# Walking the adjacency matrix by 512-column chunks instead of by row strips in a four-layer graph network kernel

## The chip, the cores and the metric

The kernel runs on one core of one Trainium2 chip, in one launch. The metric is the device time of that launch in microseconds (us), as a median of several executions; 2% either way counts as a difference. Times inside a kernel come from one profiled execution each and count from the start of its span.

The engines go by their short names: PE makes the matrix products (PEld is its loading of weights) into the accumulator banks called PSUM, DVE and ACT work on vectors, POOL issues the gathers of rows here, and SP the other transfers.

## The reference

`x` has 2708 rows of 128 features, `adj` is 2708 x 2708, all float32. Cut to what matters:

```python
def layer0(x, A):                       # neighbours in feature space are added to A
    z = leaky_relu(lap_mul(A, x) @ W1 + b1)          # pass 1 over adj
    S = exp(-sqrt(dist2(z, z)) / 2); keep the 4 nearest of each row
    return lap_mul(S + A, x) @ W2 + b2               # pass 2 over adj
def layer1(X, A):                       # attention over the graph
    den = exp(leaky_relu(s_row[:, None] + s_col[None, :]))
    att = den / (A @ den)
    return A @ (att @ (X @ W))                       # a last pass over adj
layer2: normalised adj @ x, then W;  layer3: adj @ x, concat, W, relu
# each layer: x = layernorm(x + layer(x, adj))
```

The kernel computes `A @ den` cheaply: it ranks the nodes by `s_col`, and splits each row's sum by blocks of ranks into a product with block sums (the *carry* pass over adj) and a part from gathered rows of adj inside a block (the *own section*). The ranking is what end_layer0 and the rank stage below prepare.

## The kernel before: the parts concerned

The matrix is cut into 22 row tiles of 128 and 6 chunks of 512 columns (the last has 148). Six row tiles stay in the on-chip buffer (`res`), 16 are streamed again in every pass, through three buffers. Tile's scheduler decides at build time in which order each engine runs its instructions. The code is shortened, and partly put in words.

```python
def load_strip(rows):                      # 128 x 2708, 1354 KB, tag "strip", bufs=3
    s = stream.tile([P, N], F32, tag="strip", name="strip")
    nc.sync.dma_start(s[...], adjT[rows * P : ..., :])
    return s

def adj_times(y, done, extra=None, lead=()):
    accs = [acc_tile() for _ in range(C)]             # six PSUM accumulators at once
    for n, i in enumerate(streamed tiles):            # 16 strips, six products each
        src = load_strip(i)
        for c in range(C): add(c, i, src, n == 0, False)
    for c in range(C):                                # then chunk by chunk
        for i in range(S, T): add(c, i, res[:, i - S, :], ...)
        if extra is not None: extra(c, accs[c])
        nc.scalar.copy(hT[:, chunk c], accs[c])
        done(c, chunk_tiles[c])                       # work on the chunk's four node tiles

# pass 2: the 88 gathers of neighbour rows (four per node tile) and their weighted sums
for t in range(T):
    for k in range(TOPK):
        got = got_pool.tile([P, D], F32, tag="got")   # bufs=16
        nc.gpsimd.indirect_dma_start(out=got, in_=y2_rows, in_offset=where[:, t, k])
        near_sum[:, t, :] (+)= got * sim[:, t, k]     # DVE
def add_near(c, acc):  ...                            # near_sum of four tiles into acc, on PE
def end_layer0(c, ts): ...                            # linear, layernorm, scores, and the
    # masks: each tile's scores are compared with those of all earlier nodes (DVE),
    # and the masks are summed on PE into rk
adj_times(y2, end_layer0, extra=add_near)
# ... rank stage: positions, block sums lc, xws gathers, rows_from(csort), rows_from(rr) ...
# carry: six accumulators at once, evacuated at the end
# ... own section: 2 x 43 gathers of rows of adj into "strip" buffers ...
adj_times(mixed, end_layer1); adj_times(y3, end_layer2); adj_times(xs, end_layer3)
```

PSUM: 6 banks `acc` and 2 banks `mis`; `rk` takes an acc bank. Below, *end c* is end_layer0 of chunk c, timed by its first step on DVE; *rank* is the start of the rank stage; `csort` and `rr` are groups of small transposes on PE in that stage, and `xws` are rows gathered there, which ACT scales.

Of the kernel before, what the change touches and what calls it, by code (L numbers as in the profile page):

```python
# [8 lines left out]
F32 = mybir.dt.float32  # L9
# [7 lines left out]
P = 128  # L17
CW = 512
# [11 lines left out]
def kernel(  # L30
# [16 lines left out]
    nc = tc.nc  # L47
    N, D = x.shape
    assert D == P
    T = (N + P - 1) // P  # L50
    C = (N + CW - 1) // CW
    FULL = N // P
    LAST = N - FULL * P
    NQ = T
    S = T - RES
    NB = (N + BJ - 1) // BJ
    HALF = N // 2
    pw = [min(P, N - t * P) for t in range(T)]
    cw = [min(CW, N - c * CW) for c in range(C)]

    chunk_tiles = [range(c * 4, min(T, c * 4 + 4)) for c in range(C)]
# [3 lines left out]
    stream = ctx.enter_context(tc.tile_pool(name="stream", bufs=3))  # L65
    small = ctx.enter_context(tc.tile_pool(name="small", bufs=3))
    psum = ExitStack()
    acc_pool = psum.enter_context(tc.tile_pool(name="acc", bufs=6, space=bass.MemoryType.PSUM))
    mis_pool = psum.enter_context(tc.tile_pool(name="mis", bufs=2, space=bass.MemoryType.PSUM))
    dram = ctx.enter_context(tc.tile_pool(name="dram", bufs=1, space=bass.MemoryType.DRAM))  # L70

    def acc_tile():
        return acc_pool.tile([P, CW], F32, tag="acc", name="acc")
# [4 lines left out]
    def load_strip(rows):  # L78
        s = stream.tile([P, N], F32, tag="strip", name="strip")
        nc.sync.dma_start(s[: pw[rows], :], adjT[rows * P : rows * P + pw[rows], :])  # L80
        return s


    res = big.tile([P, RES, N], F32, tag="res", name="res")
# [40 lines left out]
    def evacuate(n, dst, src):  # L125
        if n % 2:
            nc.scalar.copy(dst, src)
        else:
            nc.vector.tensor_copy(dst, src)

    def adj_times(y, done, extra=None, lead=()):



        lead = dict(lead)
        accs = [acc_tile() for _ in range(C)]

        def add(c, i, src, first, last):
            nc.tensor.matmul(  # L139
                accs[c][:, : cw[c]], lhsT=y[: pw[i], i, :], rhs=src[: pw[i], c * CW : c * CW + cw[c]],  # L140
                start=first, stop=last,
            )

        for n, i in enumerate(list(lead) + [i for i in range(S) if i not in lead]):
            src = lead[i] if i in lead else load_strip(i)
            for c in range(C):
                add(c, i, src, n == 0, False)
        for c in range(C):
            for i in range(S, T):
                add(c, i, res[:, i - S, :], False, i == T - 1 and extra is None)  # L150
            if extra is not None:
                extra(c, accs[c])
            nc.scalar.copy(hT[:, c * CW : c * CW + cw[c]], accs[c][:, : cw[c]])  # L153
            done(c, chunk_tiles[c])

    def inv_sqrt(dst, src):
        nc.scalar.activation(dst, src, AF.Sqrt)
# [148 lines left out]
    with tc.tile_pool(name="knn", bufs=1) as knn:  # L306
# [46 lines left out]
        def weigh(ts):  # L353

            t0, t1 = ts[0], ts[-1] + 1
            nr, sm = near[:, t0:t1, :TOPK], sim[:, t0:t1, :]

            nc.vector.tensor_add(nr, nr, nsq[:, t0:t1, None].to_broadcast([P, t1 - t0, TOPK]))
            nc.vector.tensor_scalar(nr, nr, 0.0, DIST_EPS, op0=ALU.min, op1=ALU.subtract)
            nc.scalar.activation(sm, nr, AF.Sqrt, scale=-1.0)  # L360
            nc.scalar.activation(sm, sm, AF.Exp, scale=-0.5)
            dd = d2inv[:, t0:t1]
            nc.vector.tensor_reduce(dd, sm, AX.X, ALU.add)
            nc.vector.tensor_add(dd, dd, deg[:, t0:t1])
            inv_sqrt(dd, dd)
            scale_rows(y2, xs, d2inv, ts)
            full = min(t1, FULL)
            nc.sync.dma_start(
                y2_rows[t0 * P : full * P, :].rearrange("(t p) d -> p t d", p=P), y2[:, t0:full, :]
            )  # L370
            if full < t1:
                nc.sync.dma_start(y2_rows[FULL * P :, :], y2[:LAST, FULL, :])

        with tc.tile_pool(name="keys", bufs=3) as keys:
            for t in range(T):
                p = pw[t]
                z2 = small.tile([P, P], F32, tag="z", name="z2")
                nc.scalar.mul(z2[:, :p], zT[:, t * P : t * P + p], 2.0)

                key = keys.tile([P, N], F32, tag="key", name="key")  # L380
                pks = [acc_tile() for _ in range(C)]
                for c in range(C):
                    cs = slice(c * CW, c * CW + cw[c])
                    nc.tensor.matmul(pks[c][:p, : cw[c]], lhsT=ones3[:, :p], rhs=nsq3[:, cs], start=True, stop=False)  # L384
                for c in range(C):
                    cs = slice(c * CW, c * CW + cw[c])
                    nc.tensor.matmul(pks[c][:p, : cw[c]], lhsT=z2[:, :p], rhs=zT[:, cs], start=False, stop=True)  # L387
                    nc.scalar.copy(key[:p, cs], pks[c][:p, : cw[c]])  # L388
                nc.vector.max(near[:p, t, :], key[:p])  # L389
                nc.vector.max_index(where[:p, t, :], near[:p, t, :], key[:p])  # L390
                if t == T - 6:
                    weigh(range(0, T - 5))
            weigh(range(T - 5, T))


    wide = ctx.enter_context(tc.tile_pool(name="wide", bufs=1))
# [22 lines left out]
    def add_near(c, acc):  # L419
        ts = chunk_tiles[c]  # L420
        for t in ts:
            p = pw[t]
            o = t * P - c * CW
            nc.tensor.matmul(
                acc[:, o : o + p], lhsT=near_sum[:p, t, :], rhs=ident[:p, :p], start=False, stop=(t == ts[-1])
            )
# [14 lines left out]
    rows_d = atile([T], "rows_d")  # L441
    nc.vector.memset(rows_m, 0.0)
    add_bias(b2_sb)
    rk = None

    def end_layer0(c, ts):
        nonlocal rk
        for t in ts:
            p = pw[t]
            po = linear(t, w2_sb)  # L450
# [1 line left out]
                xs[:p, t, :], po[:p, :D], d2inv[:p, t : t + 1], xs[:p, t, :], op0=ALU.mult, op1=ALU.add  # L452
            )
        normalize(ts, xs)
        if rk is None:
            rk = acc_tile()
        for t in ts:
            p, o = pw[t], t * P
            pt = mis_tile()
# [29 lines left out]
                accum_out=rows_d[:p, t : t + 1],  # L489
            )  # L490

    adj_times(y2, end_layer0, extra=add_near)
    late.close()
    lwx = ctx.enter_context(tc.tile_pool(name="lwx", bufs=1))
    xws = lwx.tile([P, NQ, D], F32, tag="xws", name="xws")
# [164 lines left out]
                haccs[:, o:e], lhsT=xws[:p, q, :], rhs=err[:p, o:e], start=(q == 0), stop=(q == NQ - 1)  # L660
            )

    accs = [acc_tile() for _ in range(C)]
    for n, i in enumerate(range(T)):
        src = load_strip(i) if i < S else res[:, i - S, :]
        for c in range(C):
            nc.tensor.matmul(  # L667
                accs[c][: 2 * NB, : cw[c]],
                lhsT=lc[: pw[i], i, :, :].rearrange("p b s -> p (b s)"),
                rhs=src[: pw[i], c * CW : c * CW + cw[c]],  # L670
                start=(n == 0), stop=(n == T - 1),
            )
    for c in range(C):
        evacuate(c, carry[: 2 * NB, c * CW : c * CW + cw[c]], accs[c][: 2 * NB, : cw[c]])
    psum.close()
    adj_half = adjT.rearrange("n (h k) -> (n h) k", h=2)
    WIDE = 2 * CW
# [67 lines left out]
                        mix(w, q, num, h * HALF + c0, hacc[:, c0 : c0 + w], own)  # L745
                nc.scalar.copy(mT[:, h * HALF : (h + 1) * HALF], hacc[:, :HALF])

    acc_pool = ctx.enter_context(tc.tile_pool(name="acc2", bufs=6, space=bass.MemoryType.PSUM))
    mis_pool = ctx.enter_context(tc.tile_pool(name="mis2", bufs=2, space=bass.MemoryType.PSUM))

    mixed = big.tile([P, T, D], F32, tag="y", name="mixed")
    for t in range(T):
# [18 lines left out]
            nc.scalar.mul(y3[: pw[t], t, :], xs[: pw[t], t, :], dinv[: pw[t], t : t + 1])  # L771
            nc.gpsimd.tensor_add(xs[: pw[t], t, :], xs[: pw[t], t, :], bl_sb[: pw[t]])

    adj_times(mixed, end_layer1)


    own3 = big.tile([P, T, D], F32, tag="y", name="own3")
# [7 lines left out]
            )  # L785
        normalize(ts, xs)

    adj_times(y3, end_layer2)

    for t in range(T):  # L790
        p = pw[t]
# [21 lines left out]
        if t1 <= ts[-1]:  # L813
            nc.sync.dma_start(out[FULL * P :, :], last[:LAST, FULL, :])

    adj_times(xs, end_layer3)


# [32 lines left out]
```

## Time and profile before

The median was 1321.56 us (1320.59 to 1323.04). PE is busy for 83% of the profiled span, DVE for 51%, POOL for 18%. By stages (from the profiled execution of 1338.7 us):

| stage | from, us | length, us | what ends last there |
|---|---|---|---|
| degrees, pass 1, neighbour search | 0 | 365 | not changed |
| pass 2 while neighbours are gathered | 365 | 146 | the 88 gathers on POOL |
| end_layer0, six chunks | 511 | 96 | DVE and PE in turn |
| rank and carry | 607 | 156 | DVE, then PE |
| own section | 763 | 227 | PE |
| layers 1 to 3 | 990 | 347 | PE, 93 to 100% busy |

Such a table is made by looking for the first or last instruction that writes a named tile, and asking for the busy time of every engine in the stretch between. The prediction shows the lines.

### The profile page before, as it was taken

How to read it: one execution, taken by the hardware profiler on the slowest of the kernel's cores; microseconds unless marked ns; L12 is line 12 of the kernel's file. 1: busy time of each engine (PE TensorE's matmuls, PEld its weight loads, DVE VectorE, ACT ScalarE, POOL GpSimd, SP SyncE). 2: the span in 40 equal slices, each digit the busy share in tenths (PEclk: the TensorE clock that was granted, in tenths of full speed). 3: DMA queues.
4: the chain of work that ended last, by engine and by line, in shares of the span. 5: the costliest groups of instructions: out<-in, count | busy, mean ns of one | idle time of the engine just before them, and what ended most of it. 6: DMA issues, size and time to landing. Idle time of an engine off the chain costs nothing.

```text
span 1337.0 us, 10860 instructions
## 1 busy us (share of the span) xinstructions
PE 1110.0 (83%) x3635; PEld 511.7 (38%) x3635; DVE 675.9 (51%) x1349; ACT 293.5 (22%) x586; POOL 244.4 (18%) x254
## 2 busy tenths in 40 slices
PE   0028998999995357855959999999989999999997
PEld 0023443444442124532524333333334444445443
DVE  3961026899942224788410099999970032034006
ACT  0000012555500001211030156666630021001001
POOL 0000000000037771000151055556500011000000
PEclk9999998999998777856979899999989999999999
DMA  9954840000184432002536044434537826833741
GB/s 318 393 232 175 312 177 1 1 0 0 29 296 156 153 131 109 1 23 71 205 117 230 22 116 160 143 118 154 170 132 255 313 97 215 311 139 115 267 158 42
DMA packets 44731, 202.60 MB, mean 152 GB/s; under 512 B 12516, under 2 KB 22118, under 8 KB 30058
## 3 DMA queue, kind: packets, MB, share of 16 engines
q1 hardware_dynamic: 22354, 161.99, 32.8%
q0 software_dynamic: 17280, 36.31, 8.9%
q10 hardware_dynamic: 5036, 3.56, 1.0%
q8 instruction: 30, 0.49, 0.1%
q14 instruction: 31, 0.25, 0.1%
HBM read 226.07 MB, written 4.16 MB: 172 GB/s over the span
## 4 chain that ended last, share of the span: by engine, by line
PE 69%; DVE 10%; issue 6%; DMA 6%; POOL 5%; POOLq 2%; ACT 1%; another core or an unknown queue 0%; ACTq 0%; DVEq 0%; SPq 0%
PE acc L139 32%; PE num L741 7%; PE acc L667 7%; PE hacc L659 7%; PE acc L387 7%; POOL got L407 4%; DVE mask L474 2%; DMA strip<-in_adjT 2%; DVE colsum L219 2%; PE acc L384 2%; POOLq L407 2%; PE mis L205 1%; DMA xs<-in_x 1%; DVE where L390 1%; DMA res<-in_adjT 1%
## 5 line engine op out<-in xcount | busy, mean ns | idle before, releaser
L139 PE MATMUL acc<-strip,y 128*128 128x512 f32 (+1 forms) x576 | 229.9, 560 | 53.9 <-DMA strip<-in_adjT 29.6
L139 PEld LDWEIGHTS acc<-strip,y 128*128 128x128 f32 x576 | 107.1, 197 | 175.0 <-issue 138.5
L728 POOL DMA_INDIRECT rows<-in_adjT,slot_i x86 | 121.3, 1410 | 156.4 <-PE num L741 104.9
L153 ACT COPY hT<-acc 128x512 f32<-128x512 f32 (+1 forms) x30 | 16.0, 534 | 468.4 <-PE acc L139 330.2
L741 PE MATMUL num<-rows,lw 128*64 128x512 f32 (+2 forms) x516 | 116.7, 561 | 2.5 <-DVE err L652 1.5
L659 PE MATMUL hacc<-err,xws 128*128 128x512 f32 (+3 forms) x264 | 111.7, 559 | 2.2 <-DVE err L654 2.2
L387 PE MATMUL acc<-zT,z 128*128 128x512 f32 (+2 forms) x264 | 109.0, 561 | 0.0
L139 PE MATMUL acc<-res,y 128*128 128x512 f32 (+1 forms) x216 | 98.2, 562 | 2.1 <-issue 1.9
L407 POOL DMA_INDIRECT got<-y_rows,where x88 | 88.2, 1003 | 45.8 <-issue 27.2
L222 PE MATMUL mis<-ones,colsum 128*128 128x1 f32 (+1 forms) x44 | 9.3, 345 | 91.7 <-DVE colsum L219 91.7
L667 PE MATMUL acc<-strip,lc 128*86 128x512 f32 x192 | 84.3, 578 | 0.9 <-DVE lc L546 0.9
L648 ACT ACTIVATE inv<-num 128x1024 f32<-128x1024 f32 (+1 forms) x88 | 64.4, 736 | 83.7 <-PE num L741 80.2
L388 ACT COPY key<-acc 128x512 f32<-128x512 f32 (+1 forms) x132 | 67.9, 537 | 58.3 <-PE acc L387 30.7
L652 DVE TENSOR_TENSOR err<-inv,num 128x1024 f32<-128x1024 f32 (+1 forms) x88 | 74.4, 855 | 12.2 <-ACT inv L649 10.5
L139 PE MATMUL acc<-strip,xs 128*128 128x512 f32 x192 | 77.2, 544 | 0.0
L654 DVE SCALAR_TENSOR_TENSOR err<-hT,g_inv,err 128x1024 f32<-128x1024 f32 (+1 forms) x88 | 77.0, 916 | 0.0
L659 PEld LDWEIGHTS hacc<-err,xws 128*128 128x128 f32 (+1 forms) x264 | 46.5, 189 | 79.6 <-issue 45.1
L139 PE MATMUL acc<-strip,mixed 128*128 128x512 f32 x192 | 75.5, 554 | 0.0
L653 DVE SCALAR_TENSOR_TENSOR err<-err,inv 128x1024 f32<-128x1024 f32 (+1 forms) x88 | 71.8, 856 | 0.0
L387 PEld LDWEIGHTS acc<-zT,z 128*128 128x128 f32 (+1 forms) x264 | 47.7, 188 | 59.0 <-issue 58.4
L389 DVE MAX8 near<-key 128x8 f32<-128x2708 f32 (+1 forms) x22 | 65.5, 2979 | 6.1 <-ACT key L388 6.1
L649 ACT ACTIVATE inv<-inv 128x1024 f32<-128x1024 f32 (+1 forms) x88 | 67.2, 768 | 2.6
(213 smaller groups left out, 1133.6 us busy)
## 6 DMA issues: line engine op xcount, KB each, us to landing
strip<-in_adjT SPq DMA_DIRECT2D x109, 1354.0 KB
res<-in_adjT SPq DMA_DIRECT2D x5, 1354.0 KB
got<-y_rows,where POOLq DMA_INDIRECT x88
rows<-in_adjT,slot_i POOLq DMA_INDIRECT x86
rows<-carry SPq DMA_DIRECT2D x86, 10.6 KB
xw_rows<-xwe ACTq DMA_DIRECT2D x1, 1344.0 KB
out<-last SPq DMA_DIRECT2D x5, 256.0 KB
y_rows<-y SPq DMA_DIRECT2D x1, 1088.0 KB
```

Source lines behind the costliest of these rows:

```text
L139: nc.tensor.matmul(accs[c][:, : cw[c]], lhsT=y[: pw[i], i, :], rhs=src[: pw[i], c * CW : c * CW + cw[c]], start=first, stop=last,)
L387: nc.tensor.matmul(pks[c][:p, : cw[c]], lhsT=z2[:, :p], rhs=zT[:, cs], start=False, stop=True)
L388: nc.scalar.copy(key[:p, cs], pks[c][:p, : cw[c]])
L407: nc.gpsimd.indirect_dma_start(out=got[:p, :], out_offset=None, in_=y2_rows[:, :], in_offset=bass.IndirectOffsetOnAxis(ap=where[:p, t, k : ...
L649: nc.scalar.activation(inv[:p], inv[:p], AF.Exp, scale=-1.0)
L652: nc.vector.tensor_mul(err[:p], inv[:p], num[:p, :w])
L653: nc.vector.scalar_tensor_tensor(err[:p], err[:p], 2.0, inv[:p], op0=ALU.subtract, op1=ALU.mult)
L654: nc.vector.scalar_tensor_tensor(err[:p], gb[:p, col : col + w], g_inv[:p, q : q + 1], err[:p], op0=ALU.max, op1=ALU.mult)
L659: nc.tensor.matmul(haccs[:, o:e], lhsT=xws[:p, q, :], rhs=err[:p, o:e], start=(q == 0), stop=(q == NQ - 1))
L667: nc.tensor.matmul(accs[c][: 2 * NB, : cw[c]], lhsT=lc[: pw[i], i, :, :].rearrange("p b s -> p (b s)"), rhs=src[: pw[i], c * CW : c * CW + ...
L728: nc.gpsimd.indirect_dma_start(out=rows[:KC, n, :], out_offset=None, in_=adj_half[:, :], in_offset=bass.IndirectOffsetOnAxis(ap=slot_i[h][ ...
L741: nc.tensor.matmul(num[n * BJ : n * BJ + bw[b], o:e], lhsT=lw[:, b, : bw[b]], rhs=rows[:, n, c0 + o : c0 + e], start=True, stop=True,)
```

## The change

The intent: with all of a chunk's products done first, the chunk's node work can lie under the next chunk's products, instead of the six chunks' node work standing after all streamed products. Fewer accumulators are open at a time, so PSUM banks go to `mis`, whose buffers carry the small matrices between PE, ACT and DVE. With `lag=1`, end c is put behind the products of chunk c + 1. The diff is shortened.

```diff
+    def load_panel(g, c):                      # 4 row tiles x 512 columns, 1024 KB, the same buffers
+        s = stream.tile([P, 4, CW], F32, tag="strip", name="part")
+        nc.sync.dma_start(s[:, :, : cw[c]], adjT[g*4*P:(g+1)*4*P, chunk c].rearrange("(t p) k -> p t k", p=P))
+        return s
+    def by_panels(weights, done, lag=0):
+        accs = []
+        for c in range(C):
+            acc = acc_tile(); accs.append(acc)
+            for i in range(T):
+                ... src = panel or res; one product into acc ...
+            if c >= lag:
+                done(c - lag, accs[c - lag])
+        for c in range(C - lag, C):
+            done(c, accs[c])
...
-            nc.sync.dma_start(y2_rows[...], y2[...])
+            nc.scalar.dma_start(y2_rows[...], y2[...])
...
+    psum.close()                               # after the neighbour search
+    acc_pool = ... name="acc1", bufs=3         # was 6
+    mis_pool = ... name="mis1", bufs=4         # was 2
+    rk_pool = ... name="rk", bufs=1
...
-    adj_times(y2, end_layer0, extra=add_near)
+    def end_pass2(c, acc):
+        add_near(c, acc)
+        into_hT(end_layer0)(c, acc)
+    by_panels(rows_of(y2), end_pass2, lag=1)
...
-    (carry: six accumulators, 16 strips, six evacuations at the end)
+    by_panels(lambda i: lc of tile i, end_carry)          # evacuates chunk by chunk
...
-    acc2 bufs=6, mis2 bufs=2;  adj_times(mixed | y3 | xs, ...)
+    acc2 bufs=3, mis2 bufs=5;  by_panels(rows_of(mixed | y3 | xs), into_hT(...))
```

Pass 1 keeps its row strips.

More of the change, by code (lines that the diff above doesn't have):

```diff
@@ L129, in evacuate, with adj_times @@
             nc.vector.tensor_copy(dst, src)
-    def adj_times(y, done, extra=None, lead=()):
+    def adj_times(y, done, lead):
         lead = dict(lead)
@@ L149, in adj_times, with into_hT, done, rows_of @@
             for i in range(S, T):
-                add(c, i, res[:, i - S, :], False, i == T - 1 and extra is None)
-            if extra is not None:
-                extra(c, accs[c])
+                add(c, i, res[:, i - S, :], False, i == T - 1)
             nc.scalar.copy(hT[:, c * CW : c * CW + cw[c]], accs[c][:, : cw[c]])
             done(c, chunk_tiles[c])
+    def load_panel(g, c):
+        s = stream.tile([P, 4, CW], F32, tag="strip", name="part")
+        nc.sync.dma_start(
+            s[:, :, : cw[c]],
+            adjT[g * 4 * P : (g + 1) * 4 * P, c * CW : c * CW + cw[c]].rearrange("(t p) k -> p t k", p=P),
+        )
+        return s
+    def by_panels(weights, done, lag=0):
+        accs = []
+        for c in range(C):
+            w = cw[c]
+            acc = acc_tile()
+            accs.append(acc)
+            for i in range(T):
+                if i < S:
+                    if i % 4 == 0:
+                        part = load_panel(i // 4, c)
+                    src = part[:, i % 4, :w]
+                else:
+                    src = res[: pw[i], i - S, c * CW : c * CW + w]
+                lhsT = weights(i)
+                nc.tensor.matmul(
+                    acc[: lhsT.shape[-1], :w], lhsT=lhsT, rhs=src, start=(i == 0), stop=(i == T - 1 and not lag)
+                )
+            if c >= lag:
+                done(c - lag, accs[c - lag])
+        for c in range(C - lag, C):
+            done(c, accs[c])
+    def into_hT(then):
+        def done(c, acc):
+            nc.scalar.copy(hT[:, c * CW : c * CW + cw[c]], acc[:, : cw[c]])
+            then(c, chunk_tiles[c])
+        return done
+    def rows_of(y):
+        return lambda i: y[: pw[i], i, :]
     def inv_sqrt(dst, src):
@@ L367, in weigh @@
             full = min(t1, FULL)
-            nc.sync.dma_start(
+            nc.scalar.dma_start(
                 y2_rows[t0 * P : full * P, :].rearrange("(t p) d -> p t d", p=P), y2[:, t0:full, :]
@@ L371, in weigh @@
             if full < t1:
-                nc.sync.dma_start(y2_rows[FULL * P :, :], y2[:LAST, FULL, :])
+                nc.scalar.dma_start(y2_rows[FULL * P :, :], y2[:LAST, FULL, :])
         with tc.tile_pool(name="keys", bufs=3) as keys:
@@ L393 @@
             weigh(range(T - 5, T))
+    psum.close()
+    acc_pool = psum.enter_context(tc.tile_pool(name="acc1", bufs=3, space=bass.MemoryType.PSUM))
+    mis_pool = psum.enter_context(tc.tile_pool(name="mis1", bufs=4, space=bass.MemoryType.PSUM))
+    rk_pool = psum.enter_context(tc.tile_pool(name="rk", bufs=1, space=bass.MemoryType.PSUM))
     wide = ctx.enter_context(tc.tile_pool(name="wide", bufs=1))
@@ L443 @@
     add_bias(b2_sb)
-    rk = None
+    rk = rk_pool.tile([P, T], F32, tag="rk", name="rk")
     def end_layer0(c, ts):
-        nonlocal rk
         for t in ts:
@@ L454, in end_layer0 @@
         normalize(ts, xs)
-        if rk is None:
-            rk = acc_tile()
         for t in ts:
@@ L661, in mix, with end_carry @@
             )
-    accs = [acc_tile() for _ in range(C)]
-    for n, i in enumerate(range(T)):
-        src = load_strip(i) if i < S else res[:, i - S, :]
-        for c in range(C):
-            nc.tensor.matmul(
-                accs[c][: 2 * NB, : cw[c]],
-                lhsT=lc[: pw[i], i, :, :].rearrange("p b s -> p (b s)"),
-                rhs=src[: pw[i], c * CW : c * CW + cw[c]],
-                start=(n == 0), stop=(n == T - 1),
-            )
-    for c in range(C):
-        evacuate(c, carry[: 2 * NB, c * CW : c * CW + cw[c]], accs[c][: 2 * NB, : cw[c]])
+    def end_carry(c, acc):
+        evacuate(c, carry[: 2 * NB, c * CW : c * CW + cw[c]], acc[: 2 * NB, : cw[c]])
+    by_panels(lambda i: lc[: pw[i], i, :, :].rearrange("p b s -> p (b s)"), end_carry)
     psum.close()
@@ L746 @@
                 nc.scalar.copy(mT[:, h * HALF : (h + 1) * HALF], hacc[:, :HALF])
-    acc_pool = ctx.enter_context(tc.tile_pool(name="acc2", bufs=6, space=bass.MemoryType.PSUM))
-    mis_pool = ctx.enter_context(tc.tile_pool(name="mis2", bufs=2, space=bass.MemoryType.PSUM))
+    acc_pool = ctx.enter_context(tc.tile_pool(name="acc2", bufs=3, space=bass.MemoryType.PSUM))
+    mis_pool = ctx.enter_context(tc.tile_pool(name="mis2", bufs=5, space=bass.MemoryType.PSUM))
     mixed = big.tile([P, T, D], F32, tag="y", name="mixed")
@@ L772, in end_layer1 @@
             nc.gpsimd.tensor_add(xs[: pw[t], t, :], xs[: pw[t], t, :], bl_sb[: pw[t]])
-    adj_times(mixed, end_layer1)
+    by_panels(rows_of(mixed), into_hT(end_layer1))
     own3 = big.tile([P, T, D], F32, tag="y", name="own3")
@@ L786, in end_layer2 @@
         normalize(ts, xs)
-    adj_times(y3, end_layer2)
+    by_panels(rows_of(y3), into_hT(end_layer2))
     for t in range(T):
@@ L814, in end_layer3 @@
             nc.sync.dma_start(out[FULL * P :, :], last[:LAST, FULL, :])
-    adj_times(xs, end_layer3)
+    by_panels(rows_of(xs), into_hT(end_layer3))
 def kernel(**inputs):
```

## The prediction

> **What bounds the kernel now.** I first cut the trace into stages with the windows view (one core, one die, so the cores view says nothing). Columns: window, length, then busy time (count) of PE, PEld, DVE, ACT, POOL, then granted clock, DMA share, GB/s.
>
> ```profile
> 365.00:513.00 148.00, 90.78 (x212) 41.77 (x213) 44.19 (x101) 3.69 (x7) 88.45 (x89) 0.80 0.52 177
> 513.00:607.00 94.00, 69.83 (x461) 42.73 (x460) 70.09 (x217) 22.50 (x81) 0.00 (x0) 0.72 0.13 45
> 664.00:697.00 33.00, 15.68 (x62) 8.72 (x61) 9.81 (x43) 11.73 (x30) 21.71 (x22) 0.79 0.30 95
> 697.00:763.00 66.00, 65.81 (x168) 25.46 (x166) 2.02 (x3) 2.48 (x8) 6.29 (x6) 0.97 0.40 145
> 990.00:1109.00 119.00, 116.09 (x314) 53.95 (x314) 23.86 (x109) 11.36 (x28) 7.23 (x16) 0.94 0.54 200
> 1109.00:1214.00 105.00, 105.00 (x301) 50.34 (x300) 20.42 (x97) 6.33 (x18) 2.68 (x6) 1.00 0.59 212
> 1244.00:1337.00 93.00, 86.07 (x252) 41.25 (x252) 24.07 (x123) 4.45 (x12) 0.00 (x0) 0.97 0.42 150
> ```
>
> Before 365 us nothing changes (degrees, pass 1, neighbour search), nor from 763 to 990 (own section). The last three rows are layers 1 to 3: PE is busy for 98%, 100% and 93% of them, so hiding node work there can return almost nothing. What is left is 365 to 763. Pass 2 (first two rows) has two limits in turn. To 513 POOL does 88 neighbour gathers back to back; from 513 the six end_layer0 steps follow, 94/6 = 15.7 us each, while PE is busy 74% at a clock of 0.72. The timeline of DVE shows the seam:
>
> ```profile
> 509.75 0.34 DVE L415 SCALAR_TENSOR_TENSOR near_sum<-got,sim,near_sum 20x128 f32<-20x128 f32 x1 [0.79 <-DMA got<-y_rows,where]
> 510.95 0.34 DVE L415 SCALAR_TENSOR_TENSOR near_sum<-got,sim,near_sum 20x128 f32<-20x128 f32 x1 [0.86 <-DMA got<-y_rows,where]
> 515.57 0.78 DVE L451 SCALAR_TENSOR_TENSOR xs<-mis,d2inv,xs 128x128 f32<-128x128 f32 x2 [4.28 <-PE mis L205]
> ```
>
> DVE sums the gathered rows of all 22 tiles, and only then starts L451, the first DVE step of end_layer0. The gathers set that time, 1.0 us plus 0.30 us of issue each:
>
> ```profile
> 506.13 0.96 POOL L407 DMA_INDIRECT got<-y_rows,where  x1 [0.30 <-issue]
> 507.40 0.94 POOL L407 DMA_INDIRECT got<-y_rows,where  x1 [0.30 <-issue]
> 508.65 0.95 POOL L407 DMA_INDIRECT got<-y_rows,where  x1 [0.30 <-issue]
> ```
>
> In the third window row (664 to 697) PE is busy for less than half. Its timeline shows what it waits for there: a mis buffer, which ACT has to evacuate (L200) behind scalings of gathered xws rows:
>
> ```profile
> 674.95 0.70 PE L193 MATMUL mis<-ident,csort 128*128 128x128 f32 x2 [5.74 <-issue]
> 684.51 0.65 PE L193 MATMUL mis<-ident,rr 128*128 128x128 f32 x4 [2.69 <-ACT hT L200]
> 693.66 1.11 PE L193 MATMUL mis<-ident,rr 128*128 128x128 f32 x4 [7.64 <-ACT hT L200]
> ```
>
> **What the Trainium skill says.** (1) "PSUM — Partial Sum Buffer", Engine vs sequencer instructions: the queues of ScalarE, VectorE and GpSimdE are strict FIFO, and matmuls stay in program order. The trace agrees: L451 begins 4.6 us after the last near_sum, although chunk 0's sums were ready over 100 us earlier. (2) The same page, PSUM: the matmul accumulator: 8 banks of 2 KiB per partition. One 512-column f32 accumulator fills one, so row strips need six for six chunks and leave two for mis; by chunks three suffice, which frees the banks. (3) "DMA: Bandwidth & Descriptors", Specifications: full rate from 512 B, an HBM limit of about 358 GB/s per core. The packet times here say that size matters above 512 B too: 10,832 B took 0.407 us (26.6 GB/s on one engine), 2,048 B 0.116 us (17.7).
>
> **The change part by part.**
>
> *Pass 2, gathers.* The write of y2 to memory goes to ACT's queue; before it stood on SP behind a strip issued at 378.8, landed at 386.8, and the gathers began at 387.7. I take 3 us off gather start and end: **-3**.
>
> *Pass 2, end_layer0.* The static order of the changed kernel on DVE puts only end_layer0 of chunk 0 among the near_sum tiles (the last ten of them); chunks 1 to 5 still come behind the last one, at about 508. So only one of six ends is hidden: -15. Against that, products of chunks 3, 4 and 5 now lie between the steps of ends 1 to 3 in PE's order, where before only the 36 resident products (31 us) were left. A 512-column product takes 0.857 us here (one strip of 2,708 columns 4.55 to 4.81 us), so a chunk is 22 x 0.857 = 18.9 us, chunk 5 about 5.7. Eight or nine products stand, with linear, behind the last tile's step of an end, and DVE waits there. I estimate ends 1 and 2 at 15 + 12 = 27 and 26 us, and ends 3 to 5 together at 47, as before: 100 us from 511 - 3, against 95 from 511. A second seam like the one shown (4.5 us of add_near and linear between last near_sum and first L451) is left between ends 0 and 1: 100 - 95 + 4.5 = **+9.5** for the ends, so **+6.5** for pass 2 with the gathers.
>
> *Rank and carry.* With four mis buffers instead of two, PE's twelfth group of ranked rows needs ACT's 8th evacuation, not its 10th; in ACT's order that lies behind about 9 xws scalings rather than 16, and the gathers feeding these come 1.3 us apart. PE idles 33 - 15.7 = 17.3 us there, and the 66 us of products that follow run at 100%. I credit 16. Evacuating carry by chunks, not six at the end, and loading the first panel earlier give about 4: **-20**.
>
> *Own section start.* Before, strip buffers came free over 24 us before the carry pass ended, and the first gathered rows lay ready (726 to 737). Three panel buffers are now in use until 1.6 to 3.7 us before the end: **+3**.
>
> *Layers 1 to 3.* Layer 1 starts with 17 mixed transposes (991.4 to 999) through two buffers; five give **-4**. Panels: 4 tiles x 512 columns are 1,024 KB in 2,048-byte runs, at 16 x 17.7 = 283 GB/s 3.7 us, against 4 x 0.857 = 3.43 us of PE. Six resident tiles (5.1 us) per chunk make that good, so within a pass nothing stalls; at a boundary the short chunk 5 (5.7 us of PE) leaves too little time for the next three panels: an estimated 2 to 3 us each, **+5** over carry and layers. The tail after layer 3's last product (7.8 us) may lose 1.5: **-1.5**.
>
> *Sum:* 6.5 - 20 + 3 - 4 + 5 - 1.5 = -11. From 1321.6 that is 1310.6. Since the 9.5 rests on a wholly serial reading of two chunks, I shade it by 3: **1308 us**.
>
> **The rivals.**
>
> *A: the intended effect in full.* If all ends lay under products and gathers, rank could start some 76 us earlier (five more ends of 15 us), and the kernel take about 1240. For it: PE is busy 74% and DVE 75% in 513 to 607, so there is room to overlap. Against it: DVE's order. A half of it, products that fill PE's holes at no cost to the ends, is real: the five ends then take 77 us as before (529.4 to 606.8), pass 2 gives -15 - 3 and the kernel about 1285.
>
> *B: panels are bound by transfers.* If 2,048-byte runs move below the 210 GB/s that the passes use now, each of five passes becomes longer; at 180 GB/s by 105 x (210/180 - 1) = 17 us, some 80 in all: 1390. For it: 17.7 GB/s per engine is measured on other transfers, and the 592-byte runs of chunk 5 are shorter still. Against it: the average need lies 25% below 283.
>
> *C: products block the ends everywhere.* If PE's order costs each of ends 1 to 4 the 12 us that I gave to two of them, pass 2 loses 24 us more: 1332. For it: at the lower clock of that stage (0.72) a chunk is 26 us, not 19. Against it: the products keep PE busy, and a busy PE was granted more clock in every other window.
>
> *D: the mis wait only moves.* PE then waits for the xws gathers (21.7 us of POOL in that window) by another path, and the 16 us shrink to 5: 1319.
>
> **Range and chances.** 2% faster is below 1295.1, slower above 1348.0. Below 1295 needs the half of A and the carry gain together; I give 0.27 to that, with 0.02 of it for A in full. Above 1348 needs B, or C with D: 0.08. Between: 0.65. The range 1283 to 1335 goes from half A to C with the rest as summed.
>
> **What would show it.** Right: the last near_sum ends at about 508, only chunk 0's L451 steps (now at another line) lie before it, and the rank stage starts at 605 to 620; the wait of 5.7 to 7.6 us for mis buffers in the carry stage is gone or below 2 us, and the stretch from rank to own section is some 20 us shorter; layers 1 to 3 take 317 us, give or take 6, with PE at 95% or more. Wrong: a rank start before 595 (A) or after 630 (C); strip waits of over 3 us within a pass, not only at its start (B); the carry stage as long as before (D); or a stage that I held unchanged, from 763 to 990, that differs by over 5 us.

## The result, and the profile after

| | median, us | range | kernel before |
|---|---|---|---|
| changed kernel | 1326.26 | 1324.87 to 1326.66 (4 runs) | 1322.25 |
| the same later, slow chip | 1346.27 | 1340.39 to 1349.27 (4 runs) | 1341.50 |

The ratio is 1.003 (95% interval 1.0013 to 1.0047) and 1.0026 (0.9987 to 1.0064): the same within 2%, if anything a little slower. Ratios are the mean time of one kernel's fast runs over that of the other's of the same rounds, so not quite the ratio of the medians quoted.

So a change that rebuilt five of six passes moved the time by 0.3%. Beside the profile that I had predicted from, the changed kernel's profile (1326.7 us) looks 12 us faster, not slower. To tell which of the two is right I took a second profile of the kernel before, and that was the first experiment (run b_again below, 1321.7 us, a quick chip). All comparisons from here on use that one. Its windows and those of the changed kernel, at nearly the same boundaries (window, length, busy time of PE, PEld, DVE, ACT and POOL, granted clock, DMA share, GB/s). The second profile of before:

```profile
506.00:601.00 95.00, 68.89 (x451) 41.93 (x451) 71.28 (x218) 21.87 (x80) 0.00 (x0) 0.70 0.05 15
615.00:747.00 132.00, 123.18 (x396) 56.47 (x396) 34.00 (x125) 14.74 (x38) 28.28 (x28) 0.94 0.45 158
747.00:984.00 237.00, 230.09 (x800) 87.36 (x801) 217.92 (x282) 135.08 (x180) 114.94 (x80) 0.96 0.44 140
```

The changed kernel:

```profile
506.00:601.00 95.00, 73.38 (x480) 42.70 (x478) 61.22 (x176) 18.02 (x66) 0.00 (x0) 0.85 0.37 116
615.00:747.00 132.00, 121.79 (x396) 54.67 (x396) 35.44 (x128) 15.94 (x41) 26.51 (x27) 0.97 0.51 158
747.00:984.00 237.00, 227.58 (x789) 85.95 (x789) 214.15 (x270) 134.90 (x179) 114.06 (x82) 0.97 0.46 141
```

Read the first row of each (the second is the carry stage and the third the own section, where PE's busy time differs by 1.4 and 2.5 us). In both kernels the gathers are over at 506 and the rank stage begins at 600 to 602. The changed kernel does 10 us less on DVE in these 95 us (end 0 has moved out, under the gathers) and 4.5 us more on PE (products that used to be done before), and needs as long. DMA tells the same: 116 GB/s against 15, because panels are still coming in where before all strips were through.

What the path did in these 95 us is to be seen on DVE. In the second profile of before, where L451 is the first step of an end:

```profile
506.29 0.34 DVE L415 SCALAR_TENSOR_TENSOR near_sum<-got,sim,near_sum 20x128 f32<-20x128 f32 x1 [0.96 <-DMA got<-y_rows,where]
506.70 0.61 DVE L451 SCALAR_TENSOR_TENSOR xs<-mis,d2inv,xs 128x128 f32<-128x128 f32 x2
...
522.55 0.35 DVE L451 SCALAR_TENSOR_TENSOR xs<-mis,d2inv,xs 128x128 f32<-128x128 f32 x1
```

In the changed kernel L495 is the first step of an end_layer0, one entry per chunk (x4):

```profile
505.77 0.34 DVE L460 SCALAR_TENSOR_TENSOR near_sum<-got,sim,near_sum 20x128 f32<-20x128 f32 x1 [0.90 <-DMA got<-y_rows,where]
506.04 1.11 DVE L495 SCALAR_TENSOR_TENSOR xs<-mis,d2inv,xs 128x128 f32<-128x128 f32 x4
...
530.66 1.13 DVE L495 SCALAR_TENSOR_TENSOR xs<-mis,d2inv,xs 128x128 f32<-128x128 f32 x4 [9.29 <-PE mis L245]
...
555.54 1.13 DVE L495 SCALAR_TENSOR_TENSOR xs<-mis,d2inv,xs 128x128 f32<-128x128 f32 x4 [9.28 <-PE mis L245]
```

End 1 begins with the last near_sum, and ends 1 and 2 take 24.6 and 24.9 us each, with 9.3 us of waiting for PE at their ends. PE of the changed kernel meanwhile (start, length; L178 are the products, L469 add_near, L245 the linear that DVE waits for):

```profile
521.07 1.96 PE L178 MATMUL acc<-part,y 128*128 128x512 f32 x4
522.87 5.51 PE L178 MATMUL acc<-res,y 128*128 128x512 f32 x12
528.30 1.16 PE L469 MATMUL acc<-ident,near_sum 128*128 128x128 f32 x8
529.30 1.02 PE L178 MATMUL acc<-part,y 128*128 128x512 f32 x2
530.16 1.14 PE L245 MATMUL mis<-w,hT 128*128 128x128 f32 x8
```

Each product shows as two records, so these are eight products, one after the other, ahead of the add_near and linear of the next chunk; nothing on DVE runs in the meantime. In the second profile of before an end takes 13.4 to 17.9 us (first steps at 506.7, 522.5, 537.2, 552.7, 568.8, 586.7, rank at 600.1).

### The profile page after: what moved, and what is told of

The parts are those of the page before. It is cut to its first block, busy times and chain, and to the rows that moved or that the text cites. A ratio compares the mean times of both kernels' runs of the same rounds, so it can differ in the third digit from the quotient of the medians.

```text
span 1324.9 us, 10921 instructions
## 1 busy us (share of the span) xinstructions
PE 1094.7 (83%) x3635; PEld 502.8 (38%) x3635; DVE 672.9 (51%) x1349; ACT 294.2 (22%) x586; POOL 241.4 (18%) x254
## 5 line engine op out<-in xcount | busy, mean ns | idle before, releaser
L178 PE MATMUL acc<-part,y 128*128 128x512 f32 (+1 forms) x384 | 160.6, 560 | 2.2 <-DMA part<-in_adjT 1.6
L766 POOL DMA_INDIRECT rows<-in_adjT,slot_i x86 | 118.5, 1378 | 153.8 <-PE num L779 86.1
L178 PEld LDWEIGHTS acc<-part,y 128*128 128x128 f32 x384 | 67.8, 197 | 62.9 <-issue 59.2
L178 PE MATMUL acc<-part,lc 128*86 128x512 f32 (+1 forms) x192 | 79.8, 560 | 2.8 <-DVE lc L592 1.4
L138 PE MATMUL acc<-strip,y 128*128 128x512 f32 x192 | 74.8, 553 | 6.0 <-DVE y L202 6.0
L178 PE MATMUL acc<-part,xs 128*128 128x512 f32 (+1 forms) x192 | 77.9, 546 | 0.9 <-DMA part<-in_adjT 0.9
L189 ACT COPY hT<-acc 128x512 f32<-128x512 f32 (+1 forms) x24 | 12.8, 535 | 294.3 <-PE acc L178 235.5
L178 PE MATMUL acc<-part,mixed 128*128 128x512 f32 (+1 forms) x192 | 75.5, 545 | 0.9 <-DMA part<-in_adjT 0.9
```

What stands on the lines that cost most here:

```text
L138: nc.tensor.matmul(accs[c][:, : cw[c]], lhsT=y[: pw[i], i, :], rhs=src[: pw[i], c * CW : c * CW + cw[c]], start=first, stop=last,)
L178: nc.tensor.matmul(acc[: lhsT.shape[-1], :w], lhsT=lhsT, rhs=src, start=(i == 0), stop=(i == T - 1 and not lag))
L766: nc.gpsimd.indirect_dma_start(out=rows[:KC, n, :], out_offset=None, in_=adj_half[:, :], in_offset=bass.IndirectOffsetOnAxis(ap=slot_i[h][ ...
```

## The experiments

An edit that undoes or adds one part of the change is described by the part.

### b_again: the kernel before, profiled a second time

No edit.

> The kernel before, unchanged, for a second profile. Its profiled execution took 1338.7 us, 17 us longer than its timed ones (1320.6 to 1323.0); that of the changed kernel did not differ (1326.7 against 1324.9 to 1326.7). Theory 1 (the idle time of PE in the rank and carry stage is not always there): a second profile of about 1322 us shows the idle stretch between the last lc and the last carry product shortened by 10 us or more, all earlier stages equal to 2 us. Theory 2 (pass 2 with its gathers is what varies): rank starts 10 us or more earlier than at 607 us, and the carry stage still takes 141 us. Theory 3 (the profiler slows it each time): 1335 us or more again.

Measured: 1324.03 us (1321.69 to 1325.43), ratio 1.0017 to itself, interval 0.9981 to 1.0054; profiled execution 1321.7 us. Theory 3 falls. The two profiles of one and the same kernel differ by 17 us: the rank stage starts at 600.1 instead of 607.0 (the 88 gathers take 114.5 us from first to last instead of 121.9), and the stretch from the last lc to the last carry product takes 132.2 us instead of 141.2. So theories 1 and 2 each had half of it. The seam of 4.3 us, which I had shown, is 0.1 us here. And the waits of PE for mis buffers, in this execution:

```profile
661.67 0.65 PE L193 MATMUL mis<-ident,csort 128*128 128x128 f32 x4 [0.67 <-ACT hT L200]
667.57 0.70 PE L193 MATMUL mis<-ident,csort 128*128 128x128 f32 x2 [5.25 <-ACT hT L200]
677.44 0.65 PE L193 MATMUL mis<-ident,rr 128*128 128x128 f32 x4 [1.14 <-ACT hT L200]
680.00 0.70 PE L193 MATMUL mis<-ident,rr 128*128 128x128 f32 x2 [1.66 <-ACT hT L200]
```

8.7 us, where the first profile has 17.3. In the first one ACT began to scale a tile of xws up to 10.4 us after POOL was done with its gather, here at most 4.8. The first profile is no accident: both marks come back, with the kernel before at 1341 us. There the 88 gathers take 122.2 and 122.3 us (e_carry_mis2, a_again), and with row strips and two mis buffers PE's waits in the csort and rr groups sum to 16.4 and 18.0 us (n_rows, n_rows_2). The kernel before itself was not profiled on those chips.

### e_pass2, e_carry, e_layers: one part of the change each

The edits: the kernel before, plus `load_panel` and `by_panels`, used in pass 2 only (banks 3 + 4 + 1 there, back to 6 + 2 from the rank stage on), in carry only (banks 3 + 4 from the rank stage on), and in layers 1 to 3 only (banks 3 + 5).

> Only pass 2 by panels (with its lag, and banks 3 + 4 + 1 for this pass alone); carry and layers by row strips as before; y2 rows written from the SP queue as before. Theory 1: -5 to 0 us in the timed runs, as the two profiles' rank starts (607.0 and 601.5) differ. Theory 2: +5 to +12, since the pass before is faster in timed runs than its profile says.

> Only the carry products by panels, with 3 acc and 4 mis banks from the rank stage on; all else as before. My prediction's step: -20. The two profiles: -11 (141.1 to 130.1 us from lc to last carry product) and about +4 at the start of the own section, so -7. Theory 1 (the idle time is not there in timed runs): between -3 and +5.

> Only layers 1 to 3 by panels, with 3 acc and 5 mis banks there. My prediction's steps: -4 for the transposes of mixed, +4 for pass boundaries, -1.5 for the tail: -1.5. The two profiles: 344.3 and 341.5 us from the last hacc to the end: -3. If panels cost more than thought: +3 or more.

| run | median, us | ratio | interval | in its profile, against b_again |
|---|---|---|---|---|
| e_pass2 | 1324.61 | 1.003 | 0.9989 to 1.007 | rank +1.1, end +0.7 |
| e_carry | 1320.91 | 0.9983 | 0.9946 to 1.002 | last lc to last carry product 129.3 against 132.2; own section starts 3.0 after it against 0.0, and takes 231.2 against 226.1; end +5.2 |
| e_layers | 1321.83 | 1.0016 | 0.997 to 1.0061 | mixed -3.4, tail -1.2, passes +2.3; end -2.2 |

No part moves the time beyond its interval. Theory 1's bound held for carry. The profiled execution of e_carry is the longest of its four (1326.9 us against 1318.1 to 1321.2), so its +5.2 is not how the kernel usually ran. The layers' sum in the profile (-2.2 us) is near my -1.5 for the three terms there, but the timed runs don't resolve it.

The carry stage is where my largest term was. The changed kernel's waits for mis buffers, with four of them:

```profile
663.21 0.65 PE L233 MATMUL mis<-ident,rr 128*128 128x128 f32 x4 [0.87 <-ACT hT L240]
666.39 0.65 PE L233 MATMUL mis<-ident,rr 128*128 128x128 f32 x4 [1.68 <-ACT hT L240]
668.64 0.65 PE L233 MATMUL mis<-ident,rr 128*128 128x128 f32 x4 [0.73 <-ACT hT L240]
670.45 0.65 PE L233 MATMUL mis<-ident,rr 128*128 128x128 f32 x4 [1.17 <-ACT hT L240]
674.48 0.48 PE L233 MATMUL mis<-ident,rr 128*128 128x128 f32 x2 [2.52 <-ACT hT L240]
```

7.0 us, against 8.7. PE passes the csort group without a wait now, and then waits for ACT in the rr group, which comes in smaller pieces. ACT goes at the pace of the xws gathers between its evacuations, as before: the wait moved, as rival D of the prediction had it.

### e_carry_mis2: the banks taken away from e_carry

The edit: `mis` bufs 4 to 2 in e_carry. On a slow chip.

> e_carry with 2 mis banks instead of 4: what the banks alone are worth in the carry stage. My prediction's step said 16 us. In the profiles PE is idle there for 7.8 us in the second profile of before and about 7 in the changed kernel (waits for ACT, which waits for the xws gathers). If the banks only move that wait, the stretch from last lc to last carry product is within 3 us of e_carry's 129.3; if they are worth 16, it is 140 or more.

Measured: 1348.39 us, once, no interval (before: 1340.90). From last lc to last carry product 142.4 us, which by the letter of the expectation says 16 us; but the expectation compared it with a kernel on a quick chip. The right partners are the slow chip's: 134.9 us in the changed kernel there (run a_again, four mis buffers), and 141.2 with strips and two. PE's waits in the two groups are 14.6 us here and 5.6 in a_again. So the banks may be worth about 7 us on a slow chip, and about 3 us (132.2 to 129.3, with the panels) on a quick one. I take no more from this run.

### e_queue: the write of y2 from ACT's queue, alone

The edit: the two `nc.sync.dma_start(y2_rows...)` to `nc.scalar.dma_start` in the kernel before.

> The kernel before, with only the writes of y2 rows moved from SP's queue to ACT's. My prediction's step: gathers start and end 3 us earlier, -3. The profiles of the changed kernel and of the second profile of before: the first gather 15.7 us after the search's last step instead of 18.4, but that last step 2.1 us later (374.2 against 372.1). If the queue change causes both (ACT's in-order queue holds the search's copies behind the issue), the gain is 0 to -1.

Measured: 1321.75 us, ratio 0.9999, interval 0.9958 to 1.004. The first gather begins at 390.4 (b_again 390.5) and the last ends at 505.0 (504.9). The term is 0. The traces show why: the last rows of y2 were never held up on SP. They are issued as soon as DVE has made them (L162), from SP's queue in b_again (the first two lines) as from ACT's in e_queue (the third), and the first gather follows 7.6 and 7.4 us later:

```profile
382.00 0.83 DVE L162 TENSOR_TENSOR y<-xs,d2inv 128x640 f32<-128x640 f32 x1
382.86 0.38 SPq L368 DMA_DIRECT2D y_rows<-y  x1
383.00 0.38 ACTq L368 DMA_DIRECT2D y_rows<-y  x1
```

The 18.4 and 15.7 us of the expectation were counted from different steps of the search. Its last step starts at 375.1 in b_again and 375.2 in e_queue, so the queue moves neither the search nor the gathers.

### e_lag0: each chunk's end behind its own products

Two theories were left of why the gain of pass 2 does not come. **D**: DVE runs its instructions in the order that was fixed at build time, and what stands behind the last near_sum is exposed, whatever PE could overlap. **P**: PE's products are the path, and hiding ends only shifts products behind them.

```diff
-    by_panels(rows_of(y2), end_pass2, lag=1)
+    by_panels(rows_of(y2), end_pass2, lag=0, more=True)   # more: the accumulator stays open for add_near
```

> The changed kernel with lag 0 instead of 1 (each chunk's end follows its own products in program order). In DVE's static order ends 0 and 1 then lie among the near_sums, end 2 comes first behind them. Theory D (DVE's order decides: what is behind the last near_sum is exposed, whatever PE could overlap): one more end of some 25 us is hidden, rank starts near 577 instead of 601 us, 1302 us, with one stretch of 25 us and then 46 between the last near_sum and rank. Theory P (PE's products are what the path is made of; hiding ends only shifts the products behind them): rank within 5 us of 601.

Measured: 1321.31 us (1314.27 to 1322.46), ratio 0.9997, interval 0.9961 to 1.0033. The profiled execution is the quickest of five. In it the first step of end 1 is at 465.2, between the near_sums, and of end 2 at 512.0, 7.8 us after the last of them (504.2). Rank starts at 594.7, 6.8 us earlier than in the changed kernel, not 24, and 2 of these because the gathers were over earlier. Undecided by its own bounds: an end of 24.9 us is hidden, as D says, but the ends behind it get longer (from end 2 to end 3 24.9 us, then 27.3 and 17.0, where the changed kernel has 15.0 and 17.5 for the last two), because products of a chunk now lie in an end that had none. That is P's half.

### n_chain: DVE's order changed, nothing else

```diff
-    for t in range(T): ... gathers and near_sum of all 22 tiles
+    def gather(ts, behind=None):               # the same instructions, for some tiles
+        ...
+            first = nc.vector.tensor_scalar_mul(g, got, sim[:p, t, 0:1])
+            if behind is not None:             # order on the same engine, no semaphore
+                tc.add_manual_dep(first.ins, behind.ins.name, NO_SYNC, reason="order")
     def end_pass2(c, acc):
         add_near(c, acc)
         into_hT(end_layer0)(c, acc)
+        if c + 2 < C:
+            gather(chunk_tiles[c + 2], ended[c])   # ended[c]: the last DVE step of end c
+    gather(range(8))
     by_panels(rows_of(y2), end_pass2, lag=1)
```

> The changed kernel, with the first near_sum of each tile of chunk c + 2 ordered on DVE behind the last step of end c, so that DVE's order is sums 0, sums 1, end 0, sums 2, end 1 and so on. Same work, same panels. Theory D: ends 0 to 3 are covered by the gathers, each taking up to 25 us with the products between its steps; rank starts between 535 and 560 us instead of 601, kernel 1260 to 1285 us. Theory P: rank stays above 590, or the gathers now wait for DVE and end 40 us later.

Measured on a quick chip: 1280.86 us (1279.16 to 1282.77), ratio **0.9692**, interval 0.9657 to 0.9728. Rank starts at 554.9 instead of 601.5. The first steps of the ends on DVE of n_chain:

```profile
431.28 1.12 DVE L500 SCALAR_TENSOR_TENSOR xs<-mis,d2inv,xs 128x128 f32<-128x128 f32 x4
...
457.07 1.13 DVE L500 SCALAR_TENSOR_TENSOR xs<-mis,d2inv,xs 128x128 f32<-128x128 f32 x4 [0.44 <-PE mis L245]
...
482.21 1.13 DVE L500 SCALAR_TENSOR_TENSOR xs<-mis,d2inv,xs 128x128 f32<-128x128 f32 x4 [5.35 <-PE mis L245]
...
507.10 1.13 DVE L500 SCALAR_TENSOR_TENSOR xs<-mis,d2inv,xs 128x128 f32<-128x128 f32 x4 [5.34 <-PE mis L245]
```

Ends 0, 1 and 2 take 25 us each, like ends 1 and 2 of the changed kernel, but they lie under the gathers, of which the last ends at 509.0 (504.4 in the changed kernel): POOL waits for DVE's first sum of a tile there by only 6.1 us in all (its other entries for DVE are pauses of 0.3 us each, as between any two gathers):

```profile
POOL got L455 <- DVE near_sum L461: 6.1, 4, 3.6
```

Behind the last gather stand 46 us instead of 97. The edit reached little else: from the gathers to the last lc, POOL's order is that of the changed kernel, ACT's differs by one instruction, and PE's in 9 of 660 records. Theory D, for a quick chip: the changed kernel had all the room that it needed, and DVE's order closed it.

### n_chain_lag0 and n_lag2: the lag varied on top of it

The edits: lag 0 in n_chain; lag 2 in n_chain, with 4 acc and 3 mis banks.

> n_chain with lag 0. End 0 can start when its own sums are there, near 412 us. Theory D: rank 0 to 15 us earlier than in n_chain, as the last chunks' products come one chunk earlier relative to the ends.

Measured: 1285.14 us on a quick chip, ratio 0.9722. Against the expectation it is 4 us slower than n_chain: end 0 starts at 417.8 but takes 35.6 us, because the sums of chunk 1 lie between its steps and come at the gathers' pace; rank is at 561.3.

> n_chain with lag 2, 4 acc and 3 mis banks. One more chunk's products are out of the way before end 0, so one end fewer has them between its steps: the ends with a chunk's products took 25 us, those without 15. Expected: rank up to 8 us earlier than in n_chain (547 to 555), 1273 to 1281 us.

Measured on a slow chip: 1319.05 us, ratio 0.9852, interval 0.9819 to 0.9885. Not the 1273 to 1281 expected: the chip was slow, and end 0 begins only at 455.7, since three chunks' products now stand ahead of its linear on PE (DVE waits 25.7 us for it). The comparison with n_chain is in n_lag2_2.

### r_chain: the order without the panels

The edit: n_chain's order on DVE in the kernel before, with row strips in all passes.

> The kernel before, row strips in all passes, with DVE's order of n_chain (sums 2 behind end 0 and so on). Tells whether the order alone would have done it. With row strips no accumulator is complete until all 16 strips are through PE, about 470 to 485 us in the profiles of before, so end 0 starts there and the gathers of chunks 2 to 5 (56 of 88, 73 us) behind it: rank near 600 or later, 1320 us or more. If panels are not needed for it: rank below 570.

Measured on a slow chip: 1331.19 us, ratio 0.9936, interval 0.9907 to 0.9965. Its gathers and the first step of its end 0 (L456 there), from the waits of POOL and the timeline of DVE:

```profile
POOL got L410 <- DVE near_sum L416: 50.2, 4, 41.5
```

```profile
479.40 0.61 DVE L456 SCALAR_TENSOR_TENSOR xs<-mis,d2inv,xs 128x128 f32<-128x128 f32 x2 [48.55 <-PE mis L205]
```

DVE waits 48.6 us for the first chunk's accumulator, the gathers wait 50 us for DVE, and the last ends at 555.7. So the order alone gives 0.6%, panels alone nothing, and both together 1.7% on a slow chip (next section) and 3.1% on a quick one. By the 2% of the metric, only the last counts as faster; 1.7% is unclear, and r_chain is the same as before. The order alone was not run on a quick chip.

### n_rows, and a_again, n_chain_2, n_rows_2, n_lag2_2 on one chip

n_rows is n_chain with the carry pass back to row strips.

> n_chain with the carry pass put back to row strips (6 acc and 2 mis banks from the rank stage on), layers 1 to 3 by panels. In the profiles the carry pass by panels is 2 to 3 us shorter, but the own section starts 3 us later behind it and takes up to 5 us longer (rows not gathered ahead). Expected: 1 to 6 us below n_chain (1275 to 1280 us).

Measured on a slow chip: 1320.31 us, ratio 0.9852, interval 0.9826 to 0.9877 (five rounds). All were run once more together, on a slow chip again.

> The changed kernel, unchanged, beside the two best variants on one chip. On a chip where before takes some 1322 us: 1326 as first measured. On one where before takes some 1340 us (its first profile, 1338.7, and the last call): the signals between engines that come late there during the gathers also hold the changed kernel's end 0 and its products, so 1335 to 1345 us, same as before.

> n_chain again, for a comparison with n_rows and n_lag2 on one chip: 0.969 of before on a chip of the first kind; 0.985 on one of the second, as n_rows and n_lag2 had there.

> n_rows again: 1 to 6 us below n_chain_2 if carry by strips is the better half; if the own section is not slower behind panels, within 1 us or above.

> n_lag2 again: on a chip of the first kind 0 to 8 us below n_chain_2 (one end fewer with products between its steps), on one of the second kind within 3 us of it.

| run | median, us | ratio | interval |
|---|---|---|---|
| a_again (changed kernel) | 1346.27 | 1.0026 | 0.9987 to 1.0064 |
| n_chain_2 | 1319.81 | 0.9827 | 0.9797 to 0.9856 |
| n_rows_2 | 1324.55 | 0.9875 | 0.9846 to 0.9904 |
| n_lag2_2 | 1324.48 | 0.9859 | 0.9826 to 0.9891 |

The changed kernel is the same as before on a slow chip too; n_chain has the lowest median of the variants there as well, though its interval overlaps that of the other two, and by the 2% it is unclear, they the same as before. n_rows is not below it: by panels the stretch from last lc to last carry product is 136.7 us, by strips 142.0, and that outweighs the 2.8 us by which the own section starts later behind panels. My expectation there was wrong, and in n_lag2's too.

Why is the gain smaller on a slow chip? There signals between engines come late while the gathers run. The waits of ACT in n_chain_2 between 430 and 545 us, and a step of end 0 on its DVE:

```profile
ACT xT L509 <- remote: 14.6, 2, 12.0
```

```profile
453.51 0.35 DVE L531 SCALAR_TENSOR_TENSOR eq<-hT,xwe,lower 128x128 f32<-128x128 f32 x1 [16.02 <-issue]
```

ACT waits 12.0 us at one place for a result of PE, for which it waited at most 1.6 us in n_chain on the quick chip, and the ends under the gathers take 32 to 41 us each instead of 25 (first steps at 433.4, 474.9, 506.5, 539.8). End 3, at the end of the gathers, takes 15 us on both. PE's transpose for that result was over at 437.2 and ACT began at 448.1, and PE itself stood idle for 9.5 us of it. What delays the signals is not shown by these runs.

## Why the prediction was right or wrong

The class was right (the same within 2%) and the time lay in the range, but the direction was not: I forecast -13 us, and it was +4. That the time lay in the range is no merit of the sum: its largest term, -20, measured -2.1. By its own steps, from the profiles of the quick chip (b_again to the changed kernel; the sum of the column is the 5.0 us by which their last instructions differ):

| step | predicted | measured |
|---|---|---|
| pass 2, up to the start of rank | +6.5 | +1.4 |
| rank and carry | -20 | -2.1 |
| own section start | +3 | +3.1 |
| own section itself | 0 | +5.2 |
| mixed transposes | -4 | -3.4 |
| passes, first mixed product to last product | +5 | +2.0 |
| tail | -1.5 | -1.2 |

**What failed is the step "rank and carry", "I credit 16".** The mechanism (a wait for mis buffers behind xws scalings) was there, but its size was read from one profile whose execution was 17 us longer than every timed one, a fact that lay before me. In an execution of the usual length the idle time was 8.7 us, not 17.3; and of those the banks returned under 2, since ACT, and behind it the gathers, still set the pace (ACT waits 17.5 us for gathered xws rows, against 15.2 before). On a slow chip, where the first profile was at home, the step (from the start of rank to the last carry product) is -6.3 (155.8 to 149.5), still far from -20. There the waits for mis buffers did shrink, from 17.3 to 5.6 us (a_again), but PE's other waits from the last lc to the last carry product, most of them between the products by panels, grew from 0.9 to 7.5 us. Rival D was the right reading of the size ("the 16 us shrink to 5"), and I gave it no weight in the sum.

**Pass 2** was right in its mechanism and nearly in its pieces: only end 0 is hidden; ends 1 and 2 take 24.6 and 24.9 us (predicted 27 and 26), ends 3 to 5 together 46.0 (47). Two sub-terms were wrong, one each way: the seam of 4.5 us, charged a second time, is 0.1 us long in an execution of usual length (on the slow chip it is there: 4.9 us in a_again), and the 3 us from the queue are 0. The reading behind these 3 us was wrong: the write did not stand behind a strip, but was issued at 379.87, when DVE had just made its rows (379.83). "A fully hidden" was rightly excluded, and n_chain shows that the reason given, DVE's order, was the right one: with the order changed rank starts 47 us earlier.

**Own section**: the later start was right to 0.1 us. That it then takes 5.2 us longer I had not foreseen, and by my own signs, a stage held unchanged that differs by over 5 us counts as wrong; the changed kernel waits for gathered rows now and then (0.9 us for rows from carry at its start, 1.3 us at 809). But over all profiled kernels the section takes 224.7 to 231.8 us behind strips and 225.6 to 232.3 behind panels, so I don't hold the 5 us to be shown as an effect of the change. Nor is it excluded: seven of the eight executions behind strips are at 226.5 or less, nine of the ten behind panels above that.

**Panels** (rival B) never bound a pass: in the changed kernel PE waits for panels for 1.6 us in pass 2 and layer 2 together, 1.3 in carry and 0.9 each in layers 1 and 3, and the passes' +2.0 are below the +5 allowed. The 17.7 GB/s that I had reckoned with was that of other transfers: the panels' own packets of 2,048 bytes took 0.084 us in the median (24.4 GB/s). On a slow chip one wait for a panel within the carry pass reached 4.7 us (n_lag2), over the 3 us that I had named as a sign of B. Rival C was right in kind for ends 1 and 2 alone, as summed.

**Layers 1 to 3** last 344 us in the changed kernel, not 317: that figure was the sum of the three window rows shown, and leaves out the 30 us from 1214 to 1244. The terms for the layers don't rest on it.

So the expected gain went to three places: the end that was hidden was given back by products, as the two ends that follow grew by 10 us each; the carry stage's idle time was half an effect of one slow execution, and for the rest it moved; and layers 1 to 3 had nothing to give, as PE was already full.

## What to carry to other kernels

When work is meant to hide under other work, look at the built order of the engine that does it: an in-order engine that has all of one kind of instruction queued first cannot hide the second kind, and ordering edges without a semaphore gave here, on top of a rebuilt data flow that alone gave nothing, 3.1% on a quick chip and 1.7% on a slow one. Without that data flow they gave 0.6% (on a slow chip). Before sizing a step by idle time in a profile, compare the profiled execution's length with the timed ones, and if it stands out, take a second profile first. And a wait for a buffer goes away only if the engine that frees it is not itself held by something slower: on the quick chip more buffers moved this one by a few instructions; on the slow one they took most of it away, and half of that came back as other waits.

## What the Trainium skill lacked or had wrong

- "PSUM — Partial Sum Buffer", Engine vs sequencer instructions, is right about FIFO queues, and that was the decisive fact; it doesn't say where the order comes from: it was fixed when the kernel was built. Here near_sums of twelve tiles were put ahead of end 0, while their gathers came only every 1.3 us; ordering edges took rank's start from 601.5 to 554.9 us.
- "DMA: Bandwidth & Descriptors", Specifications, gives an HBM limit of about 358 GB/s per core. That row is no limit for a core that streams alone, as the same page says below its table of measured bandwidths: the strips of the first profile, on one core, ran at 401 GB/s from 50 to 75 us.
- The same page and section: full rate from 512 B. In the streaming queue, the strips' packets of 10,832 bytes took 0.465 us on average (23.3 GB/s on one engine) in the kernel before, the panels' of 2,048 bytes 0.100 us (20.5 GB/s) and those of 592 bytes in the last chunk 0.038 us (15.6 GB/s) in the changed one. No pass of that profile became bound by it.
- No page gives the pace of indirect row gathers issued back to back: 1.00 us and 0.30 us of issue each here, for 128 rows of 512 bytes.
- No page says that signals between engines can come late while such gathers run: one wait of 12.0 us where the longest was 1.6 us on another chip. Whether this is what makes the kernel before 18 us longer in some calls (1323 and 1341 us) is not shown.
